# An adaLN transformer block on one core: another order of the first pair's seven products, and another queue for the second pair's tokens

## The chip, the cores and the metric

The kernel runs on one NeuronCore of a Trainium2 chip. The metric is device time in microseconds (us) for one execution of the whole program, all data in float32; lower is better. A profiled execution also gives a span, which is the time from the first to the last instruction of the program.

## What is computed

A transformer block with modulation (adaLN). Two batches of 1024 tokens with 1024 features go through attention (32 heads of 32, causal, with a linear position bias) and a gated feed-forward layer. Only the beginning matters here: the normalized and modulated tokens are multiplied with the matrix of queries, keys and values.

```python
x = L0_attn_hidden_states                      # (2, 1024, 1024)
mod = (_silu(L0_c) @ L0_wmod).reshape(L0_c.shape[0], 6, 1, -1)
sa, ca, ga, sb, cb, gb = (mod[:, 0], mod[:, 1], mod[:, 2], mod[:, 3], mod[:, 4], mod[:, 5])
...
h = _layernorm(x, axis=-1) * (1 + ca) + sa
x = x + ga * _L0_attn_ref(h, ...)
h = _layernorm(x, axis=-1) * (1 + cb) + sb
x = x + gb * _L0_ffn_ref(h, ...)

# in _L0_attn_ref
qkv = jnp.einsum('bsd,ed->bse', hidden_states, Wqkv)
qkv = jnp.clip(qkv, -CLIP_QKV, CLIP_QKV)
q, k, v = jnp.split(qkv, [D_MODEL, 2 * D_MODEL], axis=-1)
q = _layer_norm(q, q_ln_w, q_ln_b)
k = _layer_norm(k, k_ln_w, k_ln_b)
```

## The kernel before

The large matrix products are done with seven block products in place of eight (Strassen's method in Winograd's form). A product of 256 tokens ("a pair" of two tiles of 128 tokens, numbered (b, j) for the batch b and the pair j) with a weight of 1024 x 1024 is cut into halves: the tokens' operand has the blocks A11, A12, A22 and the sums S1 to S4, the weight has the blocks B11, B12, B21, B22 and the sums T1 = B12 - B11, T2 = B22 - T1, T3 = B22 - B12, T4 = B21 - T2. The seven products are listed in SEVEN (L769) in the order P1, P2, U2, P5, U3, P53, U6. Each consists of four calls of matmul (L828), which the profile shows as eight matmuls.

The products accumulate in two PSUM banks, x and y. P1, P2 and P5 start a bank afresh; the others add to what stands there. P1, U2, U3 and U6 use x; P2, P5 and P53 use y. After a product, read (L958 on) takes the bank: P1, U2 and P5 are copied by ScalarE (ACT, L961) into a tile each and left standing in the bank; P2 is added by VectorE (DVE, L968) to P1's copy and clipped (L969); P53 is added to U2's copy, U3 to P5's, and U6 is only clipped (L966). So P5, which overwrites y, waits for DVE's read of P2, and a product that adds to x or y waits for ACT's copy of what stood there.

projections (L927) runs over three parts (queries, keys, values) and, for batch 0, four pairs each. For the first part, weights_b (L789) loads four blocks of 1 MB with SyncE (SP) in the order B11, B21, B12, B22, and forms T1 and T2 on DVE (L811, L812) and T3 and T4 on GpSimd (POOL, L814, L816), in four steps each; all of them are also stored for later use (L818). B12 lies in a pool whose memory the preparation of the modulation uses first.

tokens (L902) prepares a pair: two loads of 128 x 1024 tokens by ACT's queue (L908) into the tile xt, of which there are two buffers; statistics and normalization on DVE and ACT (L709 to L727); and, put in a list of things to do, the transposes by TensorE (PE, L746), the modulation (L849 on DVE, L851 on ACT), the sums S1 to S4 (L781 to L784) and the store of the operand to memory (hop, L921, SP). The pair (0, 0) is prepared ahead; at the beginning of pair j's products the tokens of pair j + 1 are called for, so their loads wait until the transposes of pair j have freed the buffers. The list's entries are put between the products by todo.places; for the first pair from P53 on, four at a time (L956).

extra (L1486) adds other work for the first pair: vectors (L1456) loads nine small rows of scales (L1460) through ACT's queue, with an edge behind the last modulation on ACT that fixes only the order. The second batch's first pair of tokens has buffers of its own (pool "next"), and its loads too are issued by ACT (L908); they wait for the memory that the preparation used.

behind (L688) adds an edge between two instructions that the program's builder draws: where both are on one engine it says which goes first in that engine's queue, and no semaphore is waited for. Within this stage the order on an engine is chosen by the builder, not written by hand; on the chip every engine works its queue from front to back, and a DMA issue that waits holds up what stands behind it on the same engine.

Of the kernel before, what the change touches and what calls it, by code (L numbers as in the profile page):

```python
# [18 lines left out]
P = 128  # L19
# [461 lines left out]
def kernel(  # L481
# [19 lines left out]
    nc = tc.nc  # L501
    B, S, D = x.shape
    INTER = wg_t.shape[1]
    KC = D // P
    NT = S // P
# [242 lines left out]
    class Banks:  # L748
# [22 lines left out]
        ("y", "S1", "T1", "P5"), ("x", "S3", "T3", "U3"), ("y", "S4", "B22", "P53"),  # L771
        ("x", "A22", "T4", "U6"),
    )
    QUAD = {"P2": (0, 0), "P53": (0, 1), "U6": (1, 0), "U3": (1, 1)}
    MATE = {"P2": "P1", "P53": "U2", "U3": "P5"}
    SLOT = {q: i for i, q in enumerate(("A11", "A12", "S3", "A22", "S1", "S2", "S4"))}

    def sums_a(a, e0, e1):
# [4 lines left out]
        e1.tensor_sub(v["S3"], v["A11"], v["S3"])  # L783
        e1.tensor_sub(v["S4"], v["A12"], v["S2"])  # L784

    PARTS = {"T4": 0, "T1": 1, "T2": 2, "T3": 3}
    BLOCKS = {"B11": (0, 0), "B12": (0, 1), "B21": (1, 0), "B22": (1, 1)}

    def weights_b(pool, w, nm, sums, other=None, swap=False):  # L789

        made = other is None
        order = ("B11", "B21", "T2", "T1", "T3", "B22", "T4") if made else ("B11", "B21", "B12", "B22", "T1", "T2", "T3", "T4")
        bt = {
            q: (other if q == "B12" or q == "B22" and swap else pool).tile(
                [P, KC // 2, HALF], FP, tag=f"w{q}", name=f"w{q}_{nm}"
            )
            for q in order
        }  # L800
        for q in order:
            if q in BLOCKS:
                kh, n = BLOCKS[q]
                nc.sync.dma_start(
                    bt[q], w[ds(kh * D // 2, D // 2), ds(n * HALF, HALF)].rearrange("(k p) f -> p k f", p=P)
                )
            elif made:
                nc.sync.dma_start(bt[q], sums[:, PARTS[q]])
        if not made:
            for k in range(KC // 2):  # L810
                nc.vector.tensor_sub(bt["T1"][:, k], bt["B12"][:, k], bt["B11"][:, k])  # L811
                nc.vector.tensor_sub(bt["T2"][:, k], bt["B22"][:, k], bt["T1"][:, k])  # L812
            for k in range(KC // 2):
                nc.gpsimd.tensor_sub(bt["T3"][:, k], bt["B22"][:, k], bt["B12"][:, k])  # L814
            for k in range(KC // 2):
                nc.gpsimd.tensor_sub(bt["T4"][:, k], bt["B21"][:, k], bt["T2"][:, k])  # L816
            for q in ("T1", "T2", "T3", "T4"):
                nc.sync.dma_start(sums[:, PARTS[q]], bt[q])  # L818
        return bt

    def seven(a, bt, banks, read, between, grain):

        x, y = banks.pair()
        for c_, qa, qb_, q in SEVEN:
            bank = x if c_ == "x" else y
            first = q in ("P1", "P2", "P5")
            for j in range(KC // 2):
                matmul(  # L828
                    bank, a(qa, j), bt[qb_][:, j, :],
                    start=(first and j == 0), stop=(j == KC // 2 - 1), skip_group_check=True,  # L830
                )
                if j % grain == grain - 1 and j < KC // 2 - 1:
                    banks.made += 1
                    yield grain * MM
                    yield from between(q)
            read(q, bank)
            banks.made += 1
            yield grain * MM
            yield from between(q)
# [62 lines left out]
    def tokens(b, j, todo, ap_, xp, sm):  # L902

        a = ap_.tile([P, 7, KC // 2, P], FP, tag="a", name=f"a_{b}_0_{j}")
        xs = []
        for m in range(2):
            xt = xp.tile([P, D], FP, tag="xt", name=f"xt_{b}_{j}_{m}", bufs=2)
            nc.scalar.dma_start(xt, x[b, ts(2 * j + m, P), :])  # L908
            xs.append(xt)
        normalize(xs, xs, sm, f"x{b}_{j}")()  # L910
        for m in range(2):
            for g in range(2):
                def go(bank, m=m, g=g):
                    q = (("A11", "A12"), ("S3", "A22"))[m][g]
                    turned(
                        xs[m], bank, lambda k: a[:, SLOT[q], k % 4, :],
                        lambda k: modt[:, 1, k, b : b + 1], lambda k: modt[:, 0, k, b : b + 1], g,
                    )
                    if (m, g) == (1, 1):
                        sums_a(a, nc.vector, nc.gpsimd)  # L920
                        nc.sync.dma_start(hop_dram[b][j], a)  # L921
                todo.add(go)
        return a
# [3 lines left out]
    def projections(b, pools, banks, places, extra=None, other=None, side=lambda n, e: None):  # L927

        ap_, wp_, rawp, partp, qsp, xp, sm = pools
        todo = Todo(banks)
        made = {}
        if b == 0:
            made[0] = tokens(b, 0, todo, ap_, xp, sm)
        for part in range(3):
            bt = weights_b(wp_, wqkv_t[:, ts(part, D)], f"{b}_{part}", wt_dram[part], other, b == 0 and part == 1)
            for j in range(NT // 2):
                if b == 0 and part == 2 and j == NT // 4:
                    yield "mark"  # L940
                if b == 0 and part == 0:
                    if j == 0:
                        yield from todo.run(len(todo.list), True)
                    a = made.pop(j)
                    if j + 1 < NT // 2:
                        made[j + 1] = tokens(b, j + 1, todo, ap_, xp, sm)
                else:
                    a = ap_.tile([P, 7, KC // 2, P], FP, tag="a", name=f"a_{b}_{part}_{j}")
                    nc.sync.dma_start(a, hop_dram[b][j])
                if extra is not None:  # L950
                    extra(todo, part * (NT // 2) + j)
                raws = [
                    rawp.tile([P, D], FP, tag="raw", name=f"raw_{b}_{part}_{j}_{m}") for m in range(2)
                ]
                part_t = {}
                q0, n = (2 - b, places) if b or part or j else (5, 4)  # L956

                def read(q, bank):  # L958
                    if q in ("P1", "U2", "P5"):
                        part_t[q] = partp.tile([P, 512], FP, tag=q, name=f"{q}_{b}_{part}_{j}")  # L960
                        nc.scalar.copy(part_t[q], bank)  # L961
                        return
                    m, n = QUAD[q]
                    dst = raws[m][:, ts(n, HALF)]
                    if q == "U6":
                        nc.vector.tensor_scalar(dst, bank, CLIP, -CLIP, ALU.min, ALU.max)  # L966
                    else:
                        nc.vector.tensor_add(dst, part_t[MATE[q]], bank)  # L968
                        nc.vector.tensor_scalar(dst, dst, CLIP, -CLIP, ALU.min, ALU.max)  # L969

                yield from seven(
                    lambda q, i: a[:, SLOT[q], i, :], bt, banks, read, 
                    todo.places(q0, n, lambda e: side(part * (NT // 2) + j, e)), KC // 2
                )
                yield from todo.run(len(todo.list), True)
                if part == 2:
                    for m in range(2):
                        nc.sync.dma_start(v_dram[b][:, 2 * j + m, :], raws[m])
                    if j % 2:
                        ready.add((b, j // 2))  # L980
                    continue
                todo.first(normalize(raws, raws, sm, f"qk{b}_{part}_{j}"), b == 0)
                qs = qsp.tile([P, KC, 2, P], FP, tag="qs", name=f"qs_{b}_{part}_{j}")
                r_w, r_b = ((R_QW, R_QB), (R_KW, R_KB))[part]
                for m in range(2):
                    for g in range(2):
                        def go(bank, m=m, g=g, raws=raws, qs=qs, r_w=r_w, r_b=r_b, part=part, j=j):
                            turned(
                                raws[m], bank, lambda k: qs[:, k, m, :], column(vt, r_w), column(vt, r_b), g, b == 0
                            )  # L990
                            if (m, g) == (1, 1):
                                nc.sync.dma_start(
                                    qk_dram[b][part][:, :, ds(2 * j * P, 2 * P)],
                                    qs.rearrange("p k m t -> p k (m t)"),
                                )
                        todo.add(go)
# [432 lines left out]
    with ExitStack() as st:  # L1429
# [9 lines left out]
        banks = Banks(three[0:2], three[2:3] + more[2:5])  # L1439
# [136 lines left out]
    opools, _, bt, todo, _ = out_args  # L1576
# [514 lines left out]
```

## Time and profile before

| | us |
|---|---|
| median of 3 runs (2849.21 to 2854.21) | 2854.06 |
| profiled execution, its own time | 2848.94 |
| profiled execution, span | 2846.9 |
| PE busy in the span | 2691.8 (95%) |
| DVE busy | 1462.4 (51%) |
| POOL busy | 1296.2 (46%) |
| ACT busy | 687.8 (24%) |

The mean granted clock of TensorE in that execution was 0.984 of full speed. The page gives the busy time of each engine, their shares in 40 slices of the span, the DMA queues, and groups of instructions. Times in the time lines count from the start of the span. "PE" rows are matmuls, "PEld" loads of their stationary operand, a trailing "q" (ACTq, SPq) an engine's sequencer, which issues DMAs. A bracket behind a row gives the idle time of the engine before it and what ended it.

### The profile page before, as it was taken

Reading aid. Unit: us, or ns where it says so; the run is one execution under the profiler, and the core shown is the slowest. Engines: PE = TensorE matmul, PEld = TensorE weight load, DVE = VectorE, ACT = ScalarE, POOL = GpSimd, SP = SyncE. Lnnn points to the kernel's source line nnn. Section 1 sums busy time; section 2 is a strip of 40 time slices with the busy share of each in tenths; the row PEclk is TensorE's granted clock in tenths of the full one; section 3 lists DMA queues with packets and bytes.
Section 4 is the critical chain, followed back from the end, with each engine's and each line's share of the span. In section 5 each row is a group of like instructions: output and inputs, shape, how many; then the busy total and the mean of one; then the engine's idle time right before and its main releaser. Section 6 shows DMA issues by size and latency. Waiting matters only on the chain. (4 is left out here: it accounts for less than half of the span.)

```text
span 2846.9 us, 29933 instructions
## 1 busy us (share of the span) xinstructions
PE 2691.8 (95%) x10271; PEld 1328.0 (47%) x10271; DVE 1462.4 (51%) x2285; ACT 687.8 (24%) x1524; POOL 1296.2 (46%) x1270
## 2 busy tenths in 40 slices
PE   6999999999999888889999999999999998999998
PEld 2444433333333222223664444444444447888776
DVE  5766525566634457666644453544536355443442
ACT  1322243444344556554111010110101101000000
POOL 3312124545565665655447474455636431322352
PEclk9999999999999899999999999999999999999999
DMA  9877863766755554433687576675857668554552
GB/s 346 310 273 300 298 233 118 234 217 209 231 152 198 149 175 136 147 128 112 199 294 244 170 251 214 186 279 162 278 176 234 199 198 267 150 148 136 167 144 79
DMA packets 377573, 579.14 MB, mean 203 GB/s; under 512 B 21590, under 2 KB 278712, under 8 KB 366276
## 3 DMA queue, kind: packets, MB, share of 16 engines
q1 hardware_dynamic: 363928, 556.12, 59.9%
q10 hardware_dynamic: 13484, 21.02, 2.3%
q8 instruction: 84, 1.38, 0.2%
q14 instruction: 77, 0.63, 0.1%
HBM read 411.89 MB, written 165.17 MB: 203 GB/s over the span
## 5 line engine op out<-in xcount | busy, mean ns | idle before, releaser
L1069 ACT ACTIVATE p<-sc,kw 128x128 f32<-128x128 f32 (+3 forms) x1024 | 422.5, 515 | 356.9 <-PE sc L743 344.4
L743 PE MATMUL bank<-wT,a 128*128 128x512 f32 x768 | 356.8, 608 | 15.1 <-ACT P L961 8.5
L1101 POOL TENSOR_TENSOR p<-p,p 128x1024 f32<-128x1024 f32 (+3 forms) x128 | 262.5, 2051 | 174.0 <-PE av L743 142.0
L1101 DVE TENSOR_TENSOR p<-p,p 128x1024 f32<-128x1024 f32 (+3 forms) x192 | 250.2, 1314 | 143.2 <-POOL p L1073 85.2
L743 PE MATMUL bank<-wB,a 128*128 128x512 f32 x576 | 262.3, 601 | 1.4 <-DVE raw L968 0.9
L743 PE MATMUL sc<-cq,ck 32*128 32x512 f32 (+3 forms) x1536 | 192.7, 540 | 55.9 <-ACT p L1069 55.6
L743 PEld LDWEIGHTS bank<-wT,a 128*128 128x128 f32 x768 | 141.2, 193 | 190.7 <-issue 163.2
L1073 POOL TENSOR_SCALAR_AFFINE_SELECT p<-p 128x256 f32<-128x256 f32 x256 | 136.7, 548 | 195.6 <-ACT p L1069 192.2
L743 PE MATMUL av<-p,cv 128*32 128x512 f32 (+3 forms) x1536 | 170.7, 512 | 3.2 <-POOL p L1073 3.2
L743 PEld LDWEIGHTS bank<-wB,a 128*128 128x128 f32 x576 | 104.6, 190 | 144.3 <-issue 126.1
L743 PEld LDWEIGHTS sc<-cq,ck 32*128 32x128 f32 x1536 | 64.6, 186 | 193.6 <-ACT p L1069 108.0
L1863 PE MATMUL gy<-bt,sig 128*128 128x512 f32 x280 | 132.2, 594 | 7.0 <-DVE gX L1670 6.9
L1863 PE MATMUL uy<-bt,siu 128*128 128x512 f32 x280 | 131.6, 592 | 0.0
L1863 PE MATMUL gx<-bt,sig 128*128 128x512 f32 x280 | 131.6, 592 | 0.0
L1863 PE MATMUL ux<-bt,siu 128*128 128x512 f32 x280 | 131.6, 592 | 0.0
L743 PEld LDWEIGHTS av<-p,cv 128*32 128x32 f32 x1536 | 33.7, 109 | 122.5 <-issue 83.5
L1863 PEld LDWEIGHTS gy<-bt,sig 128*128 128x128 f32 x280 | 52.7, 190 | 76.1 <-issue 64.1
L1863 PEld LDWEIGHTS ux<-bt,siu 128*128 128x128 f32 x280 | 53.2, 190 | 67.0 <-issue 66.5
L1863 PEld LDWEIGHTS uy<-bt,siu 128*128 128x128 f32 x280 | 53.2, 190 | 67.0 <-issue 65.3
L1863 PEld LDWEIGHTS gx<-bt,sig 128*128 128x128 f32 x280 | 53.2, 190 | 67.0 <-issue 65.7
L1863 PE MATMUL ux<-bt,wuS 128*128 128x512 f32 x160 | 75.2, 592 | 0.0
L1863 PE MATMUL gx<-bt,wgS 128*128 128x512 f32 x160 | 75.2, 592 | 0.0
(415 smaller groups left out, 4459.8 us busy)
## 6 DMA issues: line engine op xcount, KB each, us to landing
bt<-bop_T SPq DMA_DIRECT2D x140, 512.0 KB
bt<-bop_B SPq DMA_DIRECT2D x99, 512.0 KB
a<-hop SPq DMA_DIRECT2D x20, 1792.0 KB
wm<-in_L_wmod_dram SPq DMA_DIRECT2D x48, 512.0 KB
wB<-in_L_attn_Wqkv_dram SPq DMA_DIRECT2D x21, 1024.0 KB
aq_S<-act_S SPq DMA_DIRECT2D x16, 1280.0 KB
qk<-qs SPq DMA_DIRECT2D x16, 1024.0 KB
act_S<-asS SPq DMA_DIRECT2D x30, 512.0 KB
```

What stands on the lines that cost most here:

```text
L743: return in_order(nc.tensor.matmul(*args, **kw_))
L1069: last_exp[0] = nc.scalar.activation(p[:, g, lo:hi], sp[:, g, lo:hi], AF.Exp, bias=kw[:, d, h_ : h_ + 1])
L1073: last_mask[0] = nc.gpsimd.affine_select(out=p[:, :, 0:P], in_=p[:, :, 0:P], pattern=[[0, 2], [1, P]], compare_op=ALU.is_ge, fill=0.0, bas ...
L1101: adders[b](half, jb).tensor_add(dst, dst, ps[half][:, :, 0:n])
L1863: nc.tensor.matmul(ps.rearrange("p (j t) -> p j t", j=NJ), ins[mat][qa][:, c2, :], bt[:, :, c2, :], start=(q in ("P1", "P2", "P5") and c2 ...
```

## The change

FIRST is SEVEN with the third and the fourth product exchanged: P1, P2, P5, U2, U3, P53, U6. It is used for the first pair of the first part of batch 0 alone; every other use keeps SEVEN. weights_b remembers its last load of a weight block in last_w; at the time of the second pair's tokens that is B22's load. The two loads of the second pair's tokens, (b, j) = (0, 1), are issued by SP in place of ACT, with an edge that puts them behind that load in SP's queue. The two loads of every other pair stay on ACT.

```diff
+    FIRST = tuple(SEVEN[i] for i in (0, 1, 3, 2, 4, 5, 6))
...
+    last_w = [None]
     PARTS = {"T4": 0, "T1": 1, "T2": 2, "T3": 3}
...
         for q in order:
             if q in BLOCKS:
                 kh, n = BLOCKS[q]
-                nc.sync.dma_start(
+                last_w[0] = nc.sync.dma_start(
                     bt[q], w[ds(kh * D // 2, D // 2), ds(n * HALF, HALF)].rearrange("(k p) f -> p k f", p=P)
                 )
...
-    def seven(a, bt, banks, read, between, grain):
+    def seven(a, bt, banks, read, between, grain, order=SEVEN):
 
         x, y = banks.pair()
-        for c_, qa, qb_, q in SEVEN:
+        for c_, qa, qb_, q in order:
...
             xt = xp.tile([P, D], FP, tag="xt", name=f"xt_{b}_{j}_{m}", bufs=2)
-            nc.scalar.dma_start(xt, x[b, ts(2 * j + m, P), :])
+            if (b, j) == (0, 1):
+                behind(nc.sync.dma_start(xt, x[b, ts(2 * j + m, P), :]), last_w[0])
+            else:
+                nc.scalar.dma_start(xt, x[b, ts(2 * j + m, P), :])
...
                     lambda q, i: a[:, SLOT[q], i, :], bt, banks, read, 
-                    todo.places(q0, n, lambda e: side(part * (NT // 2) + j, e)), KC // 2
+                    todo.places(q0, n, lambda e: side(part * (NT // 2) + j, e)), KC // 2,
+                    SEVEN if b or part or j else FIRST,
                 )
```

## The prediction

> **What bounds the kernel now.** I read the page first, then the time lines of TensorE (PE), ScalarE (ACT) and VectorE (DVE) over the first 66 us, then clock and DMA queues in the same stretch. The page's slices show PE full almost everywhere, with its worst slice at the start:
>
> ```profile
> PE   6999999999999888889999999999999998999998
> ```
>
> The change touches only that start. The time line of PE (start, length, engine, line, operation, count, and in brackets the idle time before it and what ended it) shows the first pair's seven products:
>
> ```profile
> 30.89 7.03 PE L743 MATMUL bank<-wB,a 128*128 128x512 f32 x16
> 46.45 12.82 PE L743 MATMUL bank<-wT,a 128*128 128x512 f32 x24 [8.53 <-ACT P L961]
> 59.10 3.60 PE L743 MATMUL bank<-wB,a 128*128 128x512 f32 x8
> 62.54 1.47 PE L746 MATMUL more<-ident,xt 128*128 128x128 f32 x12
> ```
>
> A product is 8 matmuls. P1 and P2 end at 37.92; then PE idles 8.53 us; then U2, P5, U3; P53 from 59.10; at 62.54 PE goes on to the second pair's transposes. A product at full rate takes (62.54-59.10) = 3.44 us. Whoever moves 62.54 moves the span, since PE then runs without a stop until 106.
>
> What ended the idle time was ACT's copy of P1, which stood behind nine small loads in ACT's queue:
>
> ```profile
> 39.77 0.28 ACTq L1460 DMA_DIRECT2D rows<-in_L_ffn_ad_dram  x1
> 41.81 2.36 ACTq L1460 DMA_DIRECT2D rows<-in_L_ffn_ag_dram  x2
> 44.21 1.56 ACTq L1460 DMA_DIRECT2D rows<-in_L_ffn_au_dram  x2
> 45.81 0.59 ACT L961 COPY P<-bank 128x512 f32<-128x512 f32 x1 [11.48 <-DMA rows<-in_L_ffn_au_dram]
> ```
>
> An issue here takes 0.28 us; the gap of 1.76 us behind the first is a wait for the landing of an older, unrelated transfer. The waits of SyncE's (SP) queue show that this happens in this program, where a store of activations waits for a weight's landing:
>
> ```profile
> SPq L921 <- DMA wB<-in_L_attn_Wqkv_dram: 11.3, 1, 11.3
> ```
>
> The issue at 39.77 coincides with the landing of the second pair's first tokens, below. SP's hop store waited 11.3 us from 28.75, so B12 landed at 40.0. DVE over the same time:
>
> ```profile
> 39.77 0.69 DVE L709 BATCH_NORM_STATS2 st_x<-xt 128x6 f32<-128x512 f32 x1 [3.99 <-DMA xt<-_attn_hidden_states_dram]
> 40.38 2.48 DVE L811 TENSOR_TENSOR wT<-wB,wB 128x512 f32<-128x512 f32 x4
> 42.78 1.28 DVE L709 BATCH_NORM_STATS2 st_x<-xt 128x6 f32<-128x512 f32 x2
> 44.02 6.80 DVE L812 TENSOR_TENSOR wT<-wB,wT 128x512 f32<-128x512 f32 x4
> 50.74 0.20 DVE L710 BATCH_NORM_AGGREGATE mv_x<-st_x 128x2 f32<-128x12 f32 x1
> 50.86 0.63 DVE L709 BATCH_NORM_STATS2 st_x<-xt 128x6 f32<-128x512 f32 x1
> 51.41 0.66 DVE L968 TENSOR_TENSOR raw<-P,bank 128x512 f32<-128x512 f32 x1
> ```
>
> T1 (L811) is ready at 42.86, T2 (L812) only at 50.82, and the read of P2 (L968), which frees bank y, is done at 52.07, behind T2 and the statistics. So the 8.53 us have three causes at nearly one time: P1's copy (46.40), T2's first quarter (44.02+1.75 = 45.8), and behind them P2's read.
>
> **The change, part by part.** No instruction is added or removed: the same 56 matmuls of the pair, two token loads issued by SP in place of ACT.
>
> Order of products. Now PE does P1, P2, P5, U2, U3, P53, U6. P5 starts bank y, so it waits for P2's read, which itself waits for P1's copy. Call the end of P2's read R. Before, U2 ran while R was awaited; now nothing does. From R: hand-over 0.05, four products P5, U2, U3, P53 at 3.44 (13.76). U3 follows U2 on bank x and must wait for ACT's copy of U2, formerly hidden under P5: 0.57 plus PE's drain and hand-over, about 0.17: 0.74. In the same way P5 following P2 on y is in R already. Then the clock, from the windows (PE, PEld, DVE, ACT, POOL busy, granted clock, DMA share, GB/s):
>
> ```profile
> 38.00:43.00 5.00, 0.00 (x0) 0.00 (x0) 3.23 (x6) 0.00 (x0) 0.13 (x1) 1.00 1.09 422
> 43.00:46.40 3.40, 0.00 (x0) 0.00 (x0) 3.40 (x4) 0.59 (x1) 2.41 (x2) 0.52 0.94 399
> 46.40:50.00 3.60, 3.55 (x5) 1.44 (x5) 3.60 (x3) 0.00 (x0) 3.60 (x3) 0.50 0.66 277
> 50.00:52.10 2.10, 2.00 (x5) 0.49 (x3) 2.10 (x5) 0.00 (x0) 2.10 (x3) 1.00 0.29 121
> ```
>
> After about 5 us of idleness the clock halves, and it is back 3.5 us after PE restarts. Before, that fell on U2, which crept behind T2 anyhow; now it falls on P5 and costs half of 3.5, so 1.75. Sum: second pair's transposes at R + 0.05 + 13.76 + 0.74 + 1.75 = R + 16.30. The change of the span is that less 62.54, so R - 46.24. Without the slow clock R - 47.99.
>
> When the weights land. The DMA queues in 26 to 31 us (one queue), and in 32 to 40 us (both; q1 is SP's, q10 ACT's):
>
> ```profile
> q1 hardware_dynamic: 962, 1.94, 104.4%
> ```
>
> ```profile
> q10 hardware_dynamic: 535, 1.98, 63.0%
> q1 hardware_dynamic: 593, 1.18, 39.3%
> ```
>
> Alone, weights move at 1.94/5 = 0.39 MB/us; beside tokens in ACT's queue at 1.18/8 = 0.15. ACT's 2.1 MB are two pairs: the second batch's first pair (issued 27.84, stays) and the second pair, 1.05 MB, which moves behind B22 in SP's queue. The weights are 4.19 MB; by 31.5 about 1.94+0.19 = 2.13 are through, by 35.5 another 0.59. Then the staying tokens are done and the left 1.47 MB pass by 39.3. In before the same count gives 38.4 for B12 and 42.1 for B22, which landed at 40.0 and 43.9: lag 1.6 to 1.8. So now B12 lands at about 38.2 and B22 between 39.6 and 41.1; I take 40.5, as the lag was seen both times. Tokens follow: 42.0 by the count, landed about 43.0 (42.5 to 43.8).
> The Trainium skill, DMA: Bandwidth & Descriptors, section "Issuing engines are not separate DMA queues", says that transfers run on the same 16 engines and interleave whoever issues them, which speaks against any gain here; the 1.98 against 1.18 MB above say that the queue does matter. By the page alone B22 would stay at 43.9 and the sum would be the last rival's below.
> The same page, "Where 436 GB/s comes from", lets the memory side bind at about 358 GB/s; the windows above moved 399 to 422. By the page the last 1.47 MB would take 4.1 us, and the sum would be some 0.3 us higher.
>
> SP's queue. The two issues stand behind B22's (28.75) and wait there for the transposes of the first pair to free the buffers, 31.05. Behind them on SP is the hop store, which could not start before 38.1 anyway (POOL's sums): free. If the tokens' issue slipped past 38, it would delay hop and T's stores, needed from 130 on.
>
> ACT's copy. The last small loads waited for B22's landing (43.92) and ended 1.9 us later. Now the latest of those older transfers is the second pair, 43.0; so the copy starts near 44.9 and ends at 45.5. Bounds: 44.4 to 46.4.
>
> P2's read on DVE. T2 from 40.5; 6.80 us, because POOL's T3 starts with the same landing as before: 47.3. (Alone, as T1 was, it would be 2.48; POOL's subtraction runs beside it, so I take 6.80.) The second pair's four statistics (0.63 to 0.69) and an aggregate (0.20) stood ahead of L968 before; they now become ready late, at 42 to 43, while T2 runs. R is 47.3 + 0.66 = 48.0 with none ahead, 51.0 with all. All were ahead before, but P1's copy is now done earlier against them; I take 49.7, nearer to the latter. Change +3.5, between +1.8 and +4.8. Downstream: the second pair's normalization ended at 57.99 and is needed at 66; a slip of 2 us is covered, and T4 (POOL, done about 53) is needed after 66.
>
> **Sum.** The profiled execution took 2848.94 us (span 2846.9). 2848.9 + 3.5 = 2852.4. The runs shown lie at 2849.2, 2854.1 and 2854.2, median 5.1 above the profiled one; I add half of that, 2.6, for a median of unknown kind: 2855.
>
> **Rivals.** (Times with the 2.6.)
> 1. P2's read goes ahead of T2 on DVE, which then waits for the copy. For it: L968 now releases the next product. Against: before, T2 went first although ready late. R = 45.5+0.66 = 46.2, change 0.0: 2851.5.
> 2. Faster: P1's copy gets ahead of the small loads on ACT (P1 ends at 34.5). Against: nothing in the change moves those loads; only two issues ahead of them vanish. Then P5 follows T1: 39.0 to 42.5 at full clock; U2 waits for T2's last quarter, to 48.2; 0.74; U3 and P53 to 55.8: -6.7, so 2844.8.
> 3. Slower: the statistics keep their places on DVE, one ahead of T1 and two ahead of T2, though their tokens now land later than the weights. For it: exactly this order above. Against: it was an order of arrival. T1 begins at 42.3 and T2 at 46.1 and takes 2.5 to 6.8; with 0.2+0.63+0.66 R is 50.1 to 54.4, change +3.9 to +8.2, middle +6: 2857.5. It shows as slower once R passes 52.
> 4. The change does not do what it says: the landings stay (B22 43.9). T2 ends at 50.8, R 51.5 to 54.5, change +5.3 to +8.3: 2858.3.
> Besides, later instructions may be put in another order on DVE and ACT; stalls such as 4.1 us behind L968 near 150 show its size, either sign.
>
> **How the numbers follow.** Chances: forecast 0.42, rival 1 0.12, rival 2 0.10, rival 3 0.20, rival 4 0.08, reordering 0.08. 0.2% is 5.7 us, about what a measurement of this kernel can tell from no change. Faster: 0.09 of rival 2, 0.03 of reordering: 0.12. Slower: 0.06 of the forecast (its upper end and the runs' scatter), 0.13 of rival 3, 0.07 of rival 4, 0.05 of reordering: 0.31. Within: 0.57. Range: down to 2847, leaving out most of rival 2; up to 2862, rival 3's top, 2848.9+8.2 with the median's 5.1. The forecast's own range is 2851 to 2859.
>
> **What would show it.** P5 right after P2 in PE's time line, started by DVE L968; B22 landed before 41.2 by POOL L814's start; T2 ahead of L968; a copy of P1 near 45; a gap of 0.7 us between U2 and U3; half clock under P5; transposes near 66. Wrong if P1's copy comes before 42 or L811 starts after 42, or if the first 66 us agree and the time doesn't.

## The result, and the profile after

| | before | after |
|---|---|---|
| median of the runs, us | 2850.56 (18 runs) | 2858.36 (18 runs) |
| ratio of the times, 95% interval | 1 | 1.0032 [1.0024, 1.0040] |
| profiled execution, span | 2846.9 | 2859.1 |
| mean granted clock | 0.984 | 0.980 |

The changed kernel is slower by 0.32%, about 9 us by the ratio (the medians differ by 7.8). The profiled spans differ by 12.2: before's profiled execution lies 1.6 under its median, after's 2.9 over.

In the slices of the span (row PE of the page, one digit per 71 us) the first is as full as before, since a gain and a loss fall into it, and the second is emptier, 8 for 9:

```profile
PE   6899999999999898889999999999999998999998
```

The time line of PE in the first 90 us:

```profile
30.88 7.03 PE L743 MATMUL bank<-wB,a 128*128 128x512 f32 x16
41.66 8.96 PE L743 MATMUL bank<-wT,a 128*128 128x512 f32 x16 [3.75 <-DVE raw L974]
50.46 1.02 PE L743 MATMUL bank<-wB,a 128*128 128x512 f32 x2
51.39 3.67 PE L743 MATMUL bank<-wT,a 128*128 128x512 f32 x8
...
57.48 3.60 PE L743 MATMUL bank<-wT,a 128*128 128x512 f32 x8
69.75 2.82 PE L746 MATMUL more<-ident,xt 128*128 128x128 f32 x12 [8.68 <-DVE xt L727]
...
82.53 5.37 PE L743 MATMUL bank<-wT,a 128*128 128x512 f32 x8 [2.03 <-DVE a L784]
```

PE starts again at 41.66, where it started at 46.45 before. P5 and U2 are through at 50.46, and two matmuls of P53 stand between U2 and U3. All seven products are done at 61.08. Before, U6 ended at 67.88 with 1.74 us of transposes ahead of it, so the seven products are 5.1 us earlier. Then PE stands for 8.68 us and waits for line L727, the second pair's normalization. The transposes are at 69.75 instead of 62.54.

Why PE starts earlier: ACT's time line, the first and last of the nine small loads, and the copy of P1:

```profile
33.87 0.53 ACTq L1467 DMA_DIRECT2D rows<-in_L_attn_q_ln_w_dram  x1
...
39.06 0.66 ACTq L1467 DMA_DIRECT2D rows<-in_L_ffn_au_dram  x2
39.76 0.59 ACT L967 COPY P<-bank 128x512 f32<-128x512 f32 x1 [5.44 <-DMA rows<-in_L_attn_k_ln_b_dram]
```

The copy is at 39.76, not 45.81. And on DVE (first T1, then P2's read, T2, U6's read, the statistics, the normalization of the tokens):

```profile
38.52 2.50 DVE L814 TENSOR_TENSOR wT<-wB,wB 128x512 f32<-128x512 f32 x4 [2.74 <-DMA wB<-in_L_attn_Wqkv_dram]
40.93 0.68 DVE L974 TENSOR_TENSOR raw<-P,bank 128x512 f32<-128x512 f32 x1
...
42.68 6.77 DVE L815 TENSOR_TENSOR wT<-wB,wT 128x512 f32<-128x512 f32 x4
...
61.11 0.69 DVE L972 TENSOR_SCALAR raw<-bank 128x512 f32<-128x512 f32 x1 [2.21 <-PE bank L743]
61.72 1.28 DVE L709 BATCH_NORM_STATS2 st_x<-xt 128x6 f32<-128x512 f32 x2
...
68.88 1.53 DVE L727 TENSOR_SCALAR xt<-xt,mv_x,rstd_x 128x1024 f32<-128x1024 f32 x2
```

P2's read (L974) now stands ahead of T2 (L815); it ends at 41.61 instead of 52.07. The second pair's statistics, which before stood ahead of T1, between T1 and T2 and behind T2, have moved to 61.72, behind the read of U6. There DVE had waited for PE, and it waits for no tokens: it goes from L972 to L709 without a gap.

Why the tokens are late: SP's time line (hop, the four stores of T, the two loads) and the longest waits of its queue:

```profile
39.93 0.34 SPq L927 DMA_DIRECT2D hop<-a  x1
41.20 12.16 SPq L821 DMA_DIRECT2D wt<-wT  x4
53.46 2.41 SPq L912 DMA_DIRECT2D xt<-_attn_hidden_states_dram  x2
```

```profile
SPq L821 <- DVE wT L815: 7.9, 1, 7.9
...
SPq L821 <- POOL wT L819: 2.7, 1, 2.7
```

The two loads, issued at 32.50 and 33.88 before, leave at 53.46 and 54.71. They stand behind hop and behind all four stores of the T sums, of which the second waits 7.9 us for T2 and the last 2.7 us for T4. 

The pause also slows what follows. In the windows (PE, PEld, DVE, ACT, POOL busy, granted clock, DMA share, GB/s) the clock falls to 0.50:

```profile
60.00:66.00 6.00, 1.07 (x3) 0.19 (x1) 4.89 (x10) 0.39 (x2) 2.54 (x3) 0.77 0.71 290
66.00:72.00 6.00, 2.25 (x11) 2.25 (x12) 5.86 (x18) 1.07 (x4) 2.43 (x2) 0.50 0.63 213
```

The transposes, 1.74 us before, now last 3.47 (69.75 to 73.22). Start against start, PE is 4.8 us earlier than before at the first product with a T, 7.2 later at these transposes, and (times of after) 9.6 later at 97, 15.8 at 134 and 11.5 at 164; the span is 12.2 longer. One of the stalls in between is the 2.03 us ahead of 82.53 in PE's list: it waits for the second pair's sums on DVE (L784), which stand behind statistics of the third pair:

```profile
79.49 0.69 DVE L709 BATCH_NORM_STATS2 st_x<-xt 128x6 f32<-128x512 f32 x1 [4.24 <-DMA xt<-_attn_hidden_states_dram]
```

The lateness shrinks between 134 and 164 because before loses time there. PE waits 4.12 us for a read on DVE, ahead of which DVE has waited 3.11 us for a weight of the next part, the keys; the same product in after (start 164.13) has no such wait. In before:

```profile
145.70 1.27 DVE L811 TENSOR_TENSOR wT<-wB,wB 128x512 f32<-128x512 f32 x1 [3.11 <-DMA wB<-in_L_attn_Wqkv_dram]
```

```profile
152.64 5.24 PE L743 MATMUL bank<-wT,a 128*128 128x512 f32 x8 [4.12 <-DVE raw L968]
```

So two effects of opposite sign in this stretch: some 5 us gained in the products, and more than that lost at the second pair; and further on a smaller gain, where before waits for that weight.

### The profile page after: what moved, and what is told of

Read it like the earlier page. It is cut to its first block, busy times and chain, and to the rows that moved or that the text cites. A ratio compares the mean times of both kernels' runs of the same rounds, so it can differ in the third digit from the quotient of the medians.

```text
span 2859.1 us, 29940 instructions
## 1 busy us (share of the span) xinstructions
PE 2702.3 (95%) x10271; PEld 1332.7 (47%) x10271; DVE 1462.0 (51%) x2285; ACT 688.2 (24%) x1524; POOL 1298.2 (45%) x1270
## 5 line engine op out<-in xcount | busy, mean ns | idle before, releaser
L785 POOL TENSOR_TENSOR a<-a 128x512 f32<-128x512 f32 x8 | 12.4, 1556 | 144.0 <-DVE a L783 131.3
```

## The experiments

Times in us in each kernel's profile; the ratio is against the runs of before on the same chip. "Tokens" is the issue of the second pair's first load, "P1" the start of ACT's copy of P1, "P2" the end of P2's read on DVE, "transposes" the start of the second pair's, "keys" the start of the first product with the next weight (keys), behind the four pairs of the first part; before waits 4.12 us shortly ahead of it. The first product itself starts between 30.86 and 31.32 in these traces, so differences of 0.4 us in a time mean nothing.

| kernel | tokens | P1 | P2 | transposes | keys | ratio, 95% interval |
|---|---|---|---|---|---|---|
| before | 32.50 | 45.81 | 52.07 | 62.54 | 157.72 | 1 |
| after | 53.46 | 39.76 | 41.61 | 69.75 | 168.17 | 1.0032 [1.0024, 1.0040] |
| e1: new order alone | 32.59 | 45.63 | 51.81 | 64.13 | 157.51 | 1.0007 [0.9995, 1.0019] |
| e2: SP queue alone | 53.65 | 40.27 | 41.81 | 70.78 | 165.20 | 1.0036 [1.0025, 1.0047] |
| e3: after, T stores behind the tokens | 41.35 | 39.84 | 41.77 | 58.78 | 150.58 | 0.9972 [0.9963, 0.9982] |
| e4: e3 in the old order | 41.20 | 40.30 | 41.60 | 59.03 | 148.72 | 0.9959 [0.9945, 0.9973] |
| e5: before, small loads behind P1's copy | 32.80 | 34.83 | 52.22 | 62.98 | 155.97 | 1.0001 [0.9990, 1.0013] |
| e6: e5, T2 written behind P2's read | 32.67 | 34.69 | 45.64 | 65.34 | 162.09 | 1.0022 [1.0010, 1.0034] |
| e7: e4, small loads behind P1's copy | 40.52 | 34.80 | 41.76 | 59.25 | 149.04 | 0.9984 [0.9971, 0.9996] |
| e8: e4, three T stores ahead of the tokens | 50.31 | 39.74 | 41.57 | 70.49 | 165.32 | 1.0030 [1.0015, 1.0045] |
| e9: e1, DVE's order made to fit | 32.69 | 34.72 | 43.84 | 61.95 | 154.68 | 0.9992 [0.9980, 1.0004] |
| e10: e4, hop behind the tokens | 40.39 | 40.24 | 41.55 | 59.02 | 152.08 | 0.9985 [0.9976, 0.9994] |
| e11: e4 again | 41.17 | 40.30 | 41.61 | 59.01 | 148.97 | 0.9977 [0.9966, 0.9987] |
| e12: e3 again | 41.41 | 40.35 | 41.82 | 58.51 | 150.84 | 0.9979 [0.9968, 0.9990] |

### One edit at a time (e1, e2)

e1 undoes the second edit, e2 the first:

```diff
 # e1, against after
-            if (b, j) == (0, 1):
-                behind(nc.sync.dma_start(xt, ...), last_w[0])
-            else:
-                nc.scalar.dma_start(xt, ...)
+            nc.scalar.dma_start(xt, ...)
 # e2, against after
-                    SEVEN if b or part or j else FIRST,
+                    SEVEN,
```

> The products in the new order, the second pair's tokens on ACT's queue as in before. Theory (the two edits work on different places: moving the tokens off ACT freed P1's copy, and put the tokens too late behind the stores of the T sums on SP): with the tokens back on ACT, P1's copy starts near 45.8 again and P2's read ends near 52, so P5 starts near 52, about 10 us later than in after; the second pair's transposes at 52 + 16.3 = about 68 without any 8 us wait for the normalization, and the time about 5.8 us above before (ratio 1.002). Rival (the new order of products is itself the loss, whatever the queue): the time is at or above after's (+8 to +12 us, ratio 1.003 or more) and the loss is seen within the seven products. Rival (the order itself frees P1's copy): P1's copy comes near 40 and the time is some 5 us under before (0.998).

> The second pair's tokens on SP's queue as in after, the products in the old order. Theory (late tokens are the loss): P1's copy near 40 as in after; the tokens' loads are issued at 53 to 55 behind the four stores of the T sums, the second pair's normalization ends near 70, TensorE waits 5 to 9 us for it, and the time is within 3 us of after's (ratio to before 1.002 to 1.004). Rival (the order of products is the loss): the time is not above before's (1.000 or less).

e2 is as slow as after, with the same stall ahead of the transposes:

```profile
70.78 2.82 PE L746 MATMUL more<-ident,xt 128*128 128x128 f32 x12 [7.95 <-DVE xt L727]
```

e1 is not distinguishable from before. P1's copy and P2's read are late again, as the theory said, but the price of 5.8 us did not come. PE's time line shows why:

```profile
46.27 3.78 PE L743 MATMUL bank<-wT,a 128*128 128x512 f32 x4 [8.26 <-ACT P L964]
51.86 5.42 PE L743 MATMUL bank<-wT,a 128*128 128x512 f32 x12 [1.81 <-DVE raw L971]
...
64.13 1.47 PE L746 MATMUL more<-ident,xt 128*128 128x128 f32 x12
```

In the wait for P2's read PE does not stand idle with P5 next: the builder put the first half of U2 (4 matmuls) there, though U2 is now written behind P5. The 1.6 us by which the transposes are later than before's are gone at the keys (157.51 against 157.72). So the loss is the queue's, and the order as written is only one input among others to the order that is built. The e2 kernel shows it from the other side: written U2 first, PE starts at 41.87 with work of P5, for T2, which U2 needs, is begun on DVE only at 42.88.

### The stores out of the way (e3, e4, and again e12, e11)

```diff
 # e3, against after; e4 the same with SEVEN for every pair
-            for q in ("T1", "T2", "T3", "T4"):
-                nc.sync.dma_start(sums[:, PARTS[q]], bt[q])
+            def store():
+                for q in ("T1", "T2", "T3", "T4"):
+                    nc.sync.dma_start(sums[:, PARTS[q]], bt[q])
+            if nm == "0_0":
+                stores.append(store)
+            else:
+                store()
...
                         made[j + 1] = tokens(b, j + 1, todo, ap_, xp, sm)
+                    while stores:
+                        stores.pop()()
```

> After, with the four stores of the first weights' T sums put behind the second pair's token loads in SP's queue. Theory (late tokens are the loss): the token loads are issued before 43 instead of 53.5 and land before 47, the wait of 8.68 us of TensorE for the normalization is gone or under 2 us, the second pair's transposes start at 57 to 62 instead of 69.8, and the time is 3 to 5 us under before (ratio 0.9982 to 0.999), 11 to 13 us under after. Rival (the new order of the products or what follows later in the program is the loss): the wait goes, but the time stays 5 us or more over before's (1.002 or more).

> As e3_stores_late, but with the old order of products, so that the pair e3 and e4 prices the order alone when nothing else stalls. Theory: U2 cannot run at full rate before T2 is there (about 44.4 for its first quarter, 49.5 for the last), P5 waits behind U2, so the seven products end 3 to 4 us later than in e3 (about one product of 3.44 us): the time 1 to 2 us under before (0.9993 to 1.000). Rival (the order is worth nothing, since T2 gates both): within 1 us of e3. Rival (the new order costs, by the bubble and the slow clock): under e3.

SP's queue in e3 has the loads ahead of the stores, and PE goes on to the transposes without a pause:

```profile
41.35 1.65 SPq L919 DMA_DIRECT2D xt<-_attn_hidden_states_dram  x2
43.09 10.43 SPq L824 DMA_DIRECT2D wt<-wT  x4
```

```profile
41.83 10.11 PE L743 MATMUL bank<-wT,a 128*128 128x512 f32 x16 [3.91 <-DVE raw L983]
...
58.78 1.47 PE L746 MATMUL more<-ident,xt 128*128 128x128 f32 x12
```

The pause is gone, the transposes are 3.8 us earlier than before's, and the time is 0.28% under before (8 us; 3 to 5 were expected) and, by the quotient of the two ratios, 0.6% under after. The cause of the loss is shown: the token loads' place behind the T stores. The gain over before, though, is more than the 3.8 us at the transposes. PE loses some of them again up to 112, and then wins where before waits 4.12 us; e3 waits 0.44 there and is 7.1 us ahead at the keys:

```profile
157.72 7.03 PE L743 MATMUL bank<-wB,a 128*128 128x512 f32 x16
```

```profile
150.58 7.13 PE L743 MATMUL bank<-wB,a 128*128 128x512 f32 x16 [0.44 <-DVE raw L983]
```

The first line is before's, the second e3's. So part of e3's gain comes from a later stretch that no edit here aimed at, where before's DVE waits for a weight and e3's does not. Both orders of products were run twice:

> e4 once more, beside e3 in one call: whether the old order is faster than the new one by more than the measurement's spread, as 2841.3 against 2844.5 suggested, while their profiled spans differ by 1.0 us. Theory (T2 gates both orders alike): within 2 us of e12. Rival (the new order costs): 3 us or more under e12.

> e3 once more, beside e4 in one call. Theory (T2 gates both orders alike): within 2 us of e11, 0.996 to 0.998 of before. Rival (the new order costs): 3 us or more over e11.

e3 gave 0.9972 and 0.9979, e4 0.9959 and 0.9977; the second time e12 was the faster of the two by 1.4 us in the median. The order of products as written makes no difference in time that these runs can tell, though e4 and e11 reach the keys 1.9 us ahead of e3 and e12; e4's theory, that the old order would end the products 3 to 4 us later, failed. In both, PE goes on right after P2's read and the transposes follow at 58.5 to 59.0. Against before, both versions are the faster kernel, and they beat after by more.

### How much does the lateness cost (e8, e10)

```diff
 # e8, against e4: only T4's store is held back
+            if nm == "0_0":
+                for q in ("T1", "T2", "T3"):
+                    nc.sync.dma_start(sums[:, PARTS[q]], bt[q])
 # e10, against e4: hop of pair (0, 0) goes behind the tokens too
-                        nc.sync.dma_start(hop_dram[b][j], a)
+                        if (b, j) == (0, 0):
+                            stores.append(lambda: nc.sync.dma_start(hop_dram[b][j], a))
+                        else:
+                            nc.sync.dma_start(hop_dram[b][j], a)
```

> e4 with the stores of T1, T2 and T3 ahead of the second pair's tokens and T4's alone behind them: half way between e4 and e2. Theory (the tokens are late by as much as the stores ahead of them wait): the loads are issued near 50.2 and 51.5, 3.2 us ahead of those in e2, the wait for the normalization is 3.2 us shorter than e2's 7.95 us (near 4.7 us), and the time some 3 us under e2's (ratio to before 1.002 to 1.003). Rival (only the last store, T4's, does the harm): within 2 us of e4's. Rival (the place in the queue does nothing): e2's 1.0036.

> e4 with the hop store too put behind the token loads, so that these stand directly behind B22's load in SP's queue, as the prediction had taken it. Theory: the loads are issued near 31 to 33 and the tokens land at 42.5 to 43.8 as forecast; B22 lands within 0.3 us of 41.15 all the same; the normalization ends earlier, but nothing waits for it in e4, so the time is within 1.5 us of e4's (ratio to before 0.995 to 0.9975). Rival (tokens issued early slow the weights even in the same queue): T3 on POOL starts at 42 or later and the time is 1 us or more over e4's.

e8 failed its expectation. The load left 3.3 us earlier than in e2, and nothing came of it: the pause before the transposes is 7.90 us (e2: 7.95). SP's and DVE's time lines:

```profile
50.31 2.13 SPq L924 DMA_DIRECT2D xt<-_attn_hidden_states_dram  x2
```

```profile
60.26 1.28 DVE L709 BATCH_NORM_STATS2 st_x<-xt 128x6 f32<-128x512 f32 x2
62.63 0.69 DVE L986 TENSOR_SCALAR raw<-bank 128x512 f32<-128x512 f32 x1 [1.09 <-PE bank L743]
```

The first statistics run at 60.26 without waiting for the tokens, and then DVE idles 1.09 us for U6's product before it goes on with them. So what reaches PE is not the landing itself. The loads' place makes the builder put the statistics and the normalization late in DVE's queue (e8 and e4 differ in the place of three stores alone), behind the reads of P53 or U6 and mixed with the first pair's own statistics, and DVE keeps that order though the data are there. Nor is T4's store the culprit, as the first rival had it: it stands behind the loads here. The last 3.3 us of lateness cost nothing; what costs in e8 is being planned late. No run plans the statistics early with the loads left late, so how the loss would split in after is not shown. An estimate for e8: 1.05 MB at 0.39 MB/us and a lag of 1.7, as in before, land near 54.7; statistics and normalization took 6.2 us in e10 (49.34 to 55.50), so they could have ended near 61, ahead of U6's end at 62.60.

e10 shows that the loads could not have left when the prediction said. They stand directly behind B22's load (29.82), and their buffers are free from about 31.4, when the first pair's transposes end, yet SP issues the first at 40.39, after what the profile's waits give as a wait for a transfer that has nothing to do with them:

```profile
40.39 1.14 SPq L919 DMA_DIRECT2D xt<-_attn_hidden_states_dram  x2
```

```profile
SPq L919 <- DMA rows<-in_L_attn_k_ln_w_dram: 10.1, 1, 10.1
```

The column is the wait in all, the times, and the longest. A small load of rows on ACT's queue held up SP's next issue until 40. In before and after a wait of this length (11.3 and 10.1 us) fell on hop, which nothing needed soon; in e10 it falls on the tokens. It costs nothing at the transposes, which are at 59.02 as in e4. POOL's T3 starts at 41.18, but this does not answer the rival: the tokens were issued at 40.39, when the weights had all but landed, so no run shows tokens that share SP's queue with the weights while these still move. The ratio of 0.9985 is just outside the range expected, with an interval that overlaps e11's; PE waits 2.15 us at 70.05 for a read on DVE, which it does not do in e4 or e11, and is at the keys 3.1 us behind e11.

### What the gain rests on (e5, e6, e7, e9)

e5 removes only the small loads from in front of P1's copy; e6 and e9 also write T2 behind P2's read, with the tokens left on ACT:

```diff
 # e5, against before
             def late_load(*args):
-                behind(nc.scalar.dma_start(*args), last_act[0])
+                rows_todo.append(args)
...
-                        nc.scalar.copy(part_t[q], bank)
+                        cp = nc.scalar.copy(part_t[q], bank)
+                        while rows_todo:
+                            behind(nc.scalar.dma_start(*rows_todo.pop(0)), cp)
 # e6, against e5: T2, T3, T4 and the stores in second(), called behind P2's read
+            if nm == "0_0":
+                t2_todo.append(second)
+            else:
+                second()
...
+                    if t2_todo and q == "P2":
+                        t2_todo.pop()()
 # e9, against e6: FIRST for the first pair, and the second pair's normalize behind T2
+            t2_todo.append(lambda: normalize(xs, xs, sm, f"x{b}_{j}")())
```

> Before, with the nine small loads of rows put behind ACT's copy of P1 in ACT's queue; nothing else moves. Theory (three causes ended the 8.5 us stall at nearly one time, and the one on DVE, P2's read behind T2, decided): P1's copy at 38 to 39 instead of 45.8, but TensorE starts again only with T2's first quarter near 45.8 and P5 only after P2's read near 52, so the second pair's transposes stay within 1 us of 62.54 and the time within 1 us of before (ratio 0.9996 to 1.0004). Rival (the small loads ahead of P1's copy were the price): TensorE starts again near 41, transposes near 58, 4 to 5 us under before (0.9984).

The copy of P1 moves to 34.83, eleven us earlier (38 to 39 was expected), and PE starts again 0.36 us earlier than before, released by T2:

```profile
34.83 0.59 ACT L963 COPY P<-bank 128x512 f32<-128x512 f32 x1 [0.20 <-PE bank L743]
```

```profile
46.09 13.61 PE L743 MATMUL bank<-wT,a 128*128 128x512 f32 x24 [7.87 <-DVE wT L814]
...
62.98 1.47 PE L746 MATMUL more<-ident,xt 128*128 128x128 f32 x12
```

The time is unchanged (1.0001). The copy alone was no bound; the prediction's "three causes at nearly one time" holds. What is left are T2's first quarter and P2's read behind T2; e6 and e9 try DVE's order.

> As e5, and T2, T3, T4 and their stores written behind P2's read, so that DVE reads P2 ahead of T2; the second pair's tokens stay on ACT's queue and B22 lands as in before (43.9). Theory (the gain of e3 and e4 is P2's read ahead of T2, not the earlier weights): P2's read ends near 44 to 45 (T1 to 42.9, then statistics of 0.6 each ahead of it), part of P5 runs in the former stall, and the second pair's transposes start at 58.5 to 60.5: 2 to 4 us under before (0.9986 to 0.9993). Rival (the gain needs B22 earlier): transposes within 1 us of 62.54, time within 1 us of before.

P2's read came to 45.64, somewhat behind the 44 to 45 expected, and yet the kernel became slower. DVE's time line:

```profile
44.97 0.67 DVE L980 TENSOR_TENSOR raw<-P,bank 128x512 f32<-128x512 f32 x1
...
45.68 1.30 DVE L818 TENSOR_TENSOR wT<-wB,wT 128x512 f32<-128x512 f32 x1
46.90 1.22 DVE L714 TENSOR_SCALAR ve_x<-mv_x 128x2 f32<-128x2 f32 x1
...
49.53 1.21 DVE L723 TENSOR_TENSOR fix_x<-fix_x,ve_x 128x2 f32<-128x2 f32 x1
50.67 0.68 DVE L818 TENSOR_TENSOR wT<-wB,wT 128x512 f32<-128x512 f32 x1
51.27 0.16 DVE L724 TENSOR_SCALAR fix_x<-fix_x 128x2 f32<-128x2 f32 x1
```

Between T2's first and second step stand 3.7 us of small operations of the second pair's normalization and the clip of P2's sum, which the builder filled in. T2 ends at 53.8 instead of 50.8, and U2 waits for it. Moving one read forward let other work into T2, so e6 does not separate the two theories.

> The first edit without the second: the products in the new order, the tokens on ACT's queue and landing as in before (B22 at 43.9), and DVE's work put in the order that the new product order needs: the small loads behind P1's copy, T2 written behind P2's read, the second pair's statistics behind T2. Theory (the order of work on DVE and ACT is what the early part gains by, and the weights' earlier landing is not needed for it): T1 to 42.9, P2's read ends at 43.6, all of P5 runs from there in the former stall, T2 is done near 52, U2 ends near 52.9, U3 and P53 after it, the second pair's transposes at 59.0 to 60.0 instead of 62.54: 2.5 to 3.5 us under before (0.9988 to 0.9991). Rival (the gain of e3 and e4 is B22 2.8 us earlier): transposes at 62 or later, time not under before's.

With the statistics held behind T2, P5 runs in the stall from 43.89 and the seven products get ahead of before's, by 0.6 us at the transposes; the time is 0.9992, its interval including no change. The 2.5 to 3.5 us expected there are not there; 61.95 lies nearly where the rival put it (62 or later). Part of what is missing stands in PE's and ACT's time lines:

```profile
43.89 9.42 PE L743 MATMUL bank<-wT,a 128*128 128x512 f32 x16 [5.78 <-DVE raw L984]
...
55.87 3.67 PE L743 MATMUL bank<-wT,a 128*128 128x512 f32 x8 [1.71 <-ACT U L975]
...
61.95 1.47 PE L746 MATMUL more<-ident,xt 128*128 128x128 f32 x12
```

```profile
54.72 0.29 ACT L716 ACTIVATE lv_x<-mv_x,eps_t 128x2 f32<-128x2 f32 x1 [4.24 <-DVE mv_x L710]
...
55.16 0.57 ACT L975 COPY U<-bank 128x512 f32<-128x512 f32 x1
```

U3 waits 1.71 us for ACT's copy of U2, which stands behind two small operations of the second pair's normalization that wait for DVE. The rest is T2, done at 52.1 here and at 49.59 in e3, because B22 lands later and DVE clips P2's sum in T2's midst. So the order of DVE's work alone did not bring e3's gain; how it would split between the earlier weights and the order without the 1.71 us stays open.

> e4 with the nine small loads behind P1's copy. Theory (in e4 P2's read waits for T1 on DVE, not for P1's copy): P1's copy at 38 to 38.7 instead of 40.3, P2's read still ends at 41 to 41.6, TensorE starts again within 0.6 us of e4's 41.66, time within 1 us of e4's (ratio to before 0.996). Rival (ACT's queue still holds TensorE): it starts again near 39.5 and the time is 2 us under e4's (0.9952).

In e7 P1's copy is at 34.80 and PE starts at 41.81, as in e4 (41.66): with the weights early, the read waits for T1. The trace agrees with the theory; its time of 0.9984 lies above the range expected and above e4's two runs, with an interval that overlaps both, while its profiled span (2837.6) is the shortest of all and at the keys it is level with e11 (149.04 and 148.97). I take it as no difference.

## Why the prediction was right or wrong

- **The range and the verdict.** 2858.36 lies inside 2847 to 2862, but the likeliest case, within 0.2%, did not come. Slower had 0.31. That the time lies in the range is luck: two large misses of opposite sign, the first pair's products (forecast later, in fact some 5 us earlier) and the second pair's tokens (forecast free, in fact a pause of 8.68 us), nearly cancel. By the prediction's own sign it was wrong: P1's copy came before 42. Rival 3 gave 2857.5, near the result, by a mechanism that did not occur: the statistics did not keep their places on DVE, they moved far back.
- **What bounds the kernel.** Right as far as it was tested: the copy of P1 alone was not the bound (e5).
- **Landings.** B12 right: 38.5 by the start of DVE's L814 (forecast 38.2). B22 at the upper bound: 41.2 by the start of POOL's L817 (41.21; forecast 40.5, bound 41.1). But this does not show that the other queue helps, for the tokens were in no queue then: their loads left at 53.46. The 1.05 MB that the weights did not have to share with are worth 2.7 us at 0.39 MB/us, and B22 landed 2.7 us earlier. So the rule of the Trainium skill that was weighed there (DMA: Bandwidth & Descriptors, section "Issuing engines are not separate DMA queues", transfers interleave on the same 16 engines) was not put to the test. The 1.98 against 1.18 MB that the prediction held against it are 535 and 593 packets, nearly one for one with ACT's the larger; that fits interleaving.
- **SP's queue: the step that failed.** "The two issues stand behind B22's (28.75) and wait there for the transposes of the first pair to free the buffers, 31.05", with hop behind them. The edge asks only for a place behind B22. hop and the four T stores, which are written ahead of the loads, were put ahead of them; the issue came at 53.46. And even directly behind B22 it came at 40.39 (e10). The prediction named the opposite danger, tokens delaying the stores.
- **Downstream.** "A slip of 2 us is covered": the slip was 12.4 us (normalization done at 70.4 against 57.99), and the cover ran out.
- **ACT's copy.** Forecast 44.9, bounds 44.4 to 46.4, measured 39.76. It was taken that the last small loads would wait for the tokens' landing, 43.0. They can't have waited for that, as the tokens were not yet issued; the seventh of the nine left at 38.4, when B12 landed, and the last two from 39.06 on. The copy did not set the time: DVE's T1, ahead of P2's read, ended at 41.02, after the copy's end at 40.35, and a copy 5 us earlier changed nothing (e7 beside e4).
- **P2's read.** Forecast 49.7 (bounds 48.0 to 51.0) behind T2 and the statistics; measured 41.61 ahead of T2, the order that rival 1 had (its R was 46.2). T2 itself took 6.77 us from 42.68, as forecast (6.80).
- **The sum R + 16.30.** From R = 41.61 it gives 57.9; U6, which took the place of the transposes, started at 57.48. Its parts: P5 and U2 took 8.80 us for 6.88, so 1.9 more; ACT's copy of P5 at 47.10 puts nearly all of it on P5, so on the slow clock (forecast 1.75); the 0.74 us between U2 and U3 were filled by two matmuls of P53. For e1 the sum gives 68.1 and the trace 64.13, since half of U2 ran before R: "now nothing does" was wrong there.
- **Reordering.** It had 0.08, with the 4.1 us stall near 150 as its size. That stall of before is missing in after, which wins back some 4 us there; but the order on DVE is alike in both, and what differs is that before waits for a weight's landing.

Had the loads gone ahead of the stores, the same sum with the measured R would have given 57.9 - 62.5, 4.6 us faster; e3 measured 3.8 at that place, and 0.28% (8 us) in time, which the sum does not explain.

## What to carry to other kernels

When a load is moved to another engine's queue, write down that queue as built, from the instruction it is tied to up to the next thing that waits for compute: "behind X" says nothing about what else is behind X. Ask also what the planner does with the consumers of a later load, since they may be queued late for good, even when the data arrive in time. And judge the two halves of such a change separately: here one edit gained 5 us in the products and lost more than that through stores that nothing was waiting for.

## What the runs showed of the hardware

- By the profile's waits, an issue on SP waited 10.1 us for a small load that ACT had issued (e10, L919), and in before hop waited 11.3 us for a weight that SP itself had issued: an unrelated transfer, also one of another engine, held an engine's DMA issues.
- Small DVE operations beside POOL's subtractions can be slow: 128x2 operations took 1.22 and 1.21 us in e6 (46.90 and 49.53, both in the list above) and 0.16 at 51.27, between two of POOL's (one ends at 50.73, the next starts at 51.42). Not every one is: another took 0.15 at 48.04, while POOL worked. The Trainium skill, SBUF — State Buffer, section "SBUF: two separate sides", has DVE and GpSimd share one port pair that one of them holds for a whole instruction; POOL's steps of 1.35 us in that stretch (T3, 5.38 us for four) are long enough to explain the waits, which agrees with the page but does not prove it.
- A stall of 3.75 us was enough for the clock to fall after the restart (after, first line: 0.63 in 41.6 to 46.0), not only the 8.5 us of before; around the 1.71 us of idleness in e9 (second line) it stayed at 1.00.

```profile
41.60:46.00 4.40, 4.34 (x7) 1.78 (x8) 4.37 (x4) 0.00 (x0) 4.40 (x4) 0.63 0.96 402
```

```profile
53.00:57.00 4.00, 2.29 (x6) 0.87 (x5) 3.83 (x11) 0.97 (x3) 2.70 (x3) 1.00 1.00 412
```
